# A GRU, attention and AUGRU kernel: five softmax blocks, an even pooling rate, products on GpSimd, attention ahead of the gates, and half-width chains

## The chip, the cores and the metric

The kernel runs on one core of a Trainium2 chip. The metric is the device time of one execution in microseconds (us).

Engines are named as in the profile: PE is TensorE (matmuls), PEld its weight loads, DVE is VectorE, ACT is ScalarE, POOL is GpSimd, and SP only issues transfers. "x2" behind a group is its number of instructions. An `a<-b` names the output and an input of an instruction.

## The reference, cut to what matters

A batch of 1024 histories of 100 steps goes through a GRU. All its states ("keys") are scored against one item per history by a small network. A masked softmax over the 100 steps weighs the keys into `pooled`. A second recurrence (AUGRU) runs over the keys again, its update gate scaled by `pooled`.

```python
# one GRU step
r = sigmoid(i_r + h_r); z = sigmoid(i_z + h_z); n = tanh(i_n + r * h_n)
h_new = (1.0 - z) * n + z * h
# attention over all steps
feat  = concat([keys, q, keys - q, q * keys])
score = mlp(feat, [W0, W1, W2], relu); score = where(mask == 1, score, -inf)
attn  = softmax(score, axis=1)
pooled = einsum('bt,btd->bd', attn, keys); att_seq = pooled.T[:T]
# one AUGRU step
u = a_t * sigmoid([h, x] @ Wu + bu); r = sigmoid([h, x] @ Wr + br)
h_new = (1.0 - u) * h + u * tanh([h * r, x] @ Wh + bh)
# ... masked mean of the history, then a final network of three layers
```

No AUGRU step can start before the softmax over all 100 steps is known and pooled. That is the seam in the middle of the kernel.

## The kernel before

The batch is cut in two halves of 512 columns, so that TensorE works on one half while the vector engines work on the other. A tick is one pass of the loop, with one step of each half; I call one step of one half a half-step (7.72 us of TensorE work in the GRU). The second half runs five ticks later (`LAG = 5`). Scores are collected in blocks, each with its own softmax and a running rescaling of `pooled`. After a block's softmax its rows stand in `todo`, and `pool` takes some of them in every step: a weight row and a key tile are loaded, multiplied and added.

```python
ENDS = (48, 92, T)
# ... in gru(), after the gates of a step
            d = wp.tile([P, HB], F32, name="d")
            nc.vector.tensor_sub(d, h if t else h0, pi)
            nc.vector.tensor_mul(d, pz, d)
            nc.vector.tensor_add(hn, pi, d)
            nc.gpsimd.tensor_mul(m, x, m)                    # masked history sum
            nc.gpsimd.tensor_add(hist[:, cols], hist[:, cols], m)
            nc.sync.dma_start(out=keys_d[t][:, cols], in_=hn)
# ... attend(): three matmuls a step, the second of them on kq
                kq = wp.tile([P, HB], F32, name="kq")
                nc.vector.tensor_mul(kq, self.h, item[:, self.cols])
                parts += [(wk, self.h), (wkq, kq)]
# ...
            nc.sync.dma_start(out=self.s_b[s - a0 : s - a0 + 1, :], in_=mv[SC : SC + 1, :])
            if s == ENDS[self.block] - 1:
                self.softmax()
# ... pool()
                nc.sync.dma_start(out=eb, in_=e_d[j][row, self.cols].partition_broadcast(P))
                # ...
                nc.sync.dma_start(out=k, in_=keys_d[t][:, self.cols])
                if t == 0:
                    nc.vector.tensor_mul(acc, k, eb)
                else:
                    nc.vector.tensor_mul(eb, k, eb)
                    nc.vector.tensor_add(acc, acc, eb)
# ... the loop
        for half, s in now:
            if 0 <= s < T:
                half.gru(s)
            elif T + GAP <= s < 2 * T + GAP:
                half.augru(s - T - GAP)
        for half, s in now:
            if 0 <= s < T:
                half.attend(s)
                half.pool(2 if len(half.todo) > T - s else 1)
            elif s == T:
                half.attend(T)
                half.attend(T + 1)
                half.pool(len(half.todo))
                half.weights()
```

## Time and profile before

| | before |
|---|---|
| time, median of 3 runs | 2873.81 us (2870.04 to 2875.78) |
| span of the profiled execution | 2876.6 us |
| TensorE busy | 93% |
| VectorE, GpSimd busy | 64%, 28% |

The prediction shows the lines of this profile. A busy share is read with care here. PE's busy time includes matmuls that run slowly, and their ends are modelled. So I count **TensorE loss**: the length of a stretch, less 0.4288 us for each 512-column matmul instruction in it, half of that for one of 256 columns, and 0.1 us for a transpose (two transposes in a row start 0.11 us apart in the median). The prediction took a transpose like a full instruction; that is 16 us (48 x 0.33) of the difference between its 265.7 and the 285.3 below. The other 4 us are nine instructions that lie across a cut and were counted on both sides.

### The profile page before, as it was taken

The numbers are of one execution on the slowest core, as the hardware profiler recorded it, in microseconds if no ns is written. First come the engines' busy times: TensorE is split into PE (matmuls) and PEld (weight loads), VectorE is DVE, ScalarE is ACT, GpSimd is POOL, SyncE is SP. The second block draws the span as 40 slices with busy tenths as digits, with TensorE's granted clock in tenths as the row PEclk, the third lists the DMA queues.
The fourth block names the chain that finished last, engine by engine and source line by source line (L and its number), as shares of the span: only waits on it lengthen the run. The fifth ranks groups of instructions, "written<-read, shape, count | busy, mean of one in ns | idle before, by whom it ended". The sixth has DMA issues, their size and how long they took to land.

```text
span 2876.6 us, 22338 instructions
## 1 busy us (share of the span) xinstructions
PE 2669.4 (93%) x6080; PEld 1150.3 (40%) x6080; DVE 1843.4 (64%) x2674; ACT 945.5 (33%) x1431; POOL 809.9 (28%) x615
## 2 busy tenths in 40 slices
PE   6999999999999988999998847499999999999998
PEld 2444444444434333444443312144444444444443
DVE  4666666666678998766666988655555555555553
ACT  2333333333333222333333312133333333333333
POOL 3333333333333332333332300022222222222221
PEclk8999999999999999999999978699999999999999
DMA  6332323222245777433334777733333333333331
GB/s 196 99 99 95 103 95 103 93 99 99 96 135 188 236 240 224 158 100 102 106 100 134 237 237 253 227 102 103 102 103 102 102 102 102 102 102 102 103 101 42
DMA packets 213650, 375.69 MB, mean 131 GB/s; under 512 B 31568, under 2 KB 32436, under 8 KB 213524
## 3 DMA queue, kind: packets, MB, share of 16 engines
q1 hardware_dynamic: 213524, 374.27, 40.9%
q8 instruction: 47, 0.77, 0.1%
q14 instruction: 79, 0.65, 0.1%
HBM read 320.08 MB, written 53.67 MB: 130 GB/s over the span
## 4 chain that ended last, share of the span: by engine, by line
PE 64%; DVE 20%; DMA 8%; issue 5%; ACT 3%; SPq 1%; POOL 1%; DVEq 0%; ACTq 0%; POOLq 0%
PE ps L189 18%; PE pm L237 10%; PE pu L348 6%; PE pr L348 6%; PE ph L348 6%; PE pr L350 6%; PE ph L350 6%; PE pu L350 6%; DVE d L218 3%; DMA k<-keys_d 3%; DVE hn L219 3%; DVE eb L318 3%; DMA eb<-e_d 3%; DVE u L209 2%; DVE d L217 2%
## 5 line engine op out<-in xcount | busy, mean ns | idle before, releaser
L189 PE MATMUL ps<-x,wih 128*128 128x512 f32 x1200 | 586.9, 597 | 0.0
L189 PE MATMUL ps<-hn,whh 128*128 128x512 f32 x1188 | 584.3, 599 | 1.8 <-DVE hn L219 1.8
L220 POOL TENSOR_TENSOR m<-x,m 128x512 f32<-128x512 f32 x200 | 262.7, 1313 | 1085.9 <-DMA x<-in_hist_x 1054.3
L362 POOL TENSOR_TENSOR u<-u,at 128x512 f32<-128x512 f32 x200 | 254.3, 1272 | 877.1 <-ACT u L361 865.1
L366 DVE TENSOR_TENSOR ph<-ph,hn 128x512 f32<-128x512 f32 x198 | 138.4, 699 | 450.5 <-ACT ph L364 450.3
L189 PEld LDWEIGHTS ps<-x,wih 128*128 128x128 f32 x1200 | 230.1, 192 | 291.3 <-issue 282.2
L189 PEld LDWEIGHTS ps<-hn,whh 128*128 128x128 f32 x1188 | 228.3, 192 | 289.9 <-issue 286.9
L237 PE MATMUL pm<-hn,wk 128*128 128x512 f32 x400 | 219.7, 632 | 95.0 <-DVE hn L219 94.8
L243 ACT ACTIVATE mv<-f 128x512 f32<-128x512 f32 x204 | 128.5, 630 | 540.9 <-DVE f L241 531.6
L221 POOL TENSOR_TENSOR hist<-hist,m 128x512 f32<-128x512 f32 x200 | 287.6, 1438 | 15.7
L215 ACT ACTIVATE ps<-ps,bih 128x512 f32<-128x512 f32 x200 | 132.4, 662 | 423.1 <-DVE ps L214 423.0
L348 PE MATMUL pr<-k,wr 128*128 128x512 f32 x396 | 203.4, 595 | 46.6 <-DMA k<-keys_d 46.6
L209 DVE SCALAR_TENSOR_TENSOR u<-ps,bhh,r 128x512 f32<-128x512 f32 x198 | 147.5, 745 | 144.6 <-PE ps L189 138.0
L237 PE MATMUL pm<-kq,wkq 128*128 128x512 f32 x400 | 216.5, 624 | 11.6 <-DVE kq L231 11.0
L241 DVE TENSOR_TENSOR f<-pm,q 128x512 f32<-128x512 f32 x204 | 139.7, 685 | 132.2 <-PE pm L237 132.0
L357 ACT ACTIVATE pr<-pr,br 128x512 f32<-128x512 f32 x198 | 131.1, 662 | 276.1 <-PE pr L350 276.1
L237 PE MATMUL pm<-mv,w 128*128 128x512 f32 x404 | 210.8, 604 | 2.6 <-ACT mv L243 2.6
L350 PE MATMUL pr<-hn,wr 128*128 128x512 f32 x396 | 204.1, 597 | 9.1 <-DVE hn L368 9.1
L217 DVE TENSOR_TENSOR d<-hn,ps 128x512 f32<-128x512 f32 x198 | 135.6, 685 | 115.1 <-ACT ps L215 115.1
L361 ACT ACTIVATE u<-pu,bu 128x512 f32<-128x512 f32 x200 | 137.3, 687 | 214.6 <-PE pu L350 214.6
L348 PE MATMUL pu<-k,wu 128*128 128x512 f32 x400 | 205.2, 594 | 0.0
L350 PE MATMUL ph<-r,wh 128*128 128x512 f32 x396 | 202.7, 593 | 2.4 <-DVE r L358 2.4
(93 smaller groups left out, 2936.5 us busy)
## 6 DMA issues: line engine op xcount, KB each, us to landing
k<-keys_d SPq DMA_DIRECT2D x400, 256.0 KB
eb<-e_d SPq DMA_DIRECT2D x206, 256.0 KB
x<-in_hist_x SPq DMA_DIRECT2D x200, 256.0 KB
m<-mask_d SPq DMA_DIRECT2D x200, 256.0 KB
keys_d<-hn SPq DMA_DIRECT2D x200, 256.0 KB
at<-att_d SPq DMA_DIRECT2D x200, 256.0 KB
s_b<-mv SPq DMA_DIRECT2D x200, 2.0 KB
item<-in_item SPq DMA_DIRECT2D x1, 512.0 KB
```

The costliest lines, as they stand in the source:

```text
L189: nc.tensor.matmul(p, lhsT=w[:, g, :], rhs=v, start=(n == 0), stop=(n == len(parts) - 1),)
L209: nc.vector.scalar_tensor_tensor(out=u, in0=ph, scalar=bhh[:, 2:3], in1=r, op0=ALU.add, op1=ALU.mult)
L217: nc.vector.tensor_sub(d, h if t else h0, pi)
L220: nc.gpsimd.tensor_mul(m, x, m)
L221: nc.gpsimd.tensor_add(hist[:, cols], hist[:, cols], m)
L237: nc.tensor.matmul(p, lhsT=w, rhs=v, start=(n == 0), stop=(n == len(parts) - 1))
L241: nc.vector.tensor_add(f, p, q0[:, self.cols])
L348: nc.tensor.matmul(p, lhsT=w[:, 1, :], rhs=k, start=True, stop=v is None)
L350: nc.tensor.matmul(p, lhsT=w[:, 0, :], rhs=v, start=False, stop=True)
L361: nc.scalar.activation(u, pu, AF.Sigmoid, bias=later["bu"])
L362: nc.gpsimd.tensor_mul(u, u, at)
L366: nc.vector.tensor_sub(ph, ph, h)
```

## The change

It is meant to take TensorE's idle time out of the seam and the start: five blocks that shrink, so that few rows are left when the GRU ends; rows pooled at an even rate; the row's product on GpSimd and `kq` too, to relieve VectorE; each half's attention directly ahead of its own gates; and, where one half runs alone, two chains of 256 columns.

```diff
-ENDS = (48, 92, T)
+ENDS = (44, 72, 88, 96, T)
@@ start: first weights, then the first x; reciprocals on a small tile, through memory
+    x_first = xp.tile([P, HB], F32, name="x")
+    nc.sync.dma_start(out=x_first, in_=a["hist_x"][0][:, :HB])
@@ gru(): the step's chain is run per part of the columns
+            for c in parts:
+                self.gru_chain(t, x[:, c], h[:, c] if t else h0[:, c], hn[:, c])
@@ attend()
-                nc.vector.tensor_mul(kq, self.h, item[:, self.cols])
+                nc.gpsimd.tensor_mul(kq, self.h, item[:, self.cols])
@@ pool()
-                    nc.vector.tensor_mul(eb, k, eb)
+                    nc.gpsimd.tensor_mul(eb, k, eb)
                     nc.vector.tensor_add(acc, acc, eb)
@@ the loop
+        for half, other in ((first, second), (second, first)):
+            s = tick - LAG * half.i
+            o = tick - LAG * other.i
+            alone = not (0 <= o < T or T + GAP <= o < 2 * T + GAP)
+            parts = quarters if alone else whole
+            if 1 <= s <= T:
+                half.attend(s - 1)
+            # ... last attention layers at s == T
+            if 0 <= s < T:
+                half.gru(s, parts)
+            elif T + GAP <= s < 2 * T + GAP:
+                half.augru(s - T - GAP, parts)
+            if 0 <= s < T:
+                left = next(e for e in ENDS if e > s - 2) - s + 2
+                half.pool(-(-len(half.todo) // left))
```

Cut: the augru chains, which follow the pattern of the gru's, more buffers (x 5 to 6, pooling tiles 4 to 5, own rings for AUGRU loads), and the reciprocals' transfers.

More of the change, by code (lines that the diff above doesn't have):

```diff
@@ L65 @@
     att_d = dram.tile([T, B], F32, name="att_d")
+    rlen_d = dram.tile([P, NG], F32, name="rlen_d")
     def load(name, shape, src=None, dt=F32):
@@ L73 @@
     wih = load("wih", [P, 3, P])
-    whh = load("whh", [P, 3, P])
+    xp = ctx.enter_context(tc.tile_pool(name="xp", bufs=6))
+    x_first = xp.tile([P, HB], F32, name="x")
+    nc.sync.dma_start(out=x_first, in_=a["hist_x"][0][:, :HB])
     bih = load("bih", [P, 3])
     bhh = load("bhh", [P, 3])
+    whh = load("whh", [P, 3, P])
     pre = ctx.enter_context(tc.tile_pool(name="pre", bufs=1))
@@ L120 @@
     y = const.tile([1, B], F32, name="y")
-    xp = ctx.enter_context(tc.tile_pool(name="xp", bufs=5))
     hp = ctx.enter_context(tc.tile_pool(name="hp", bufs=8))
@@ L125 @@
     sp = ctx.enter_context(tc.tile_pool(name="sp", bufs=2))
-    kp = ctx.enter_context(tc.tile_pool(name="kp", bufs=4))
+    kp = ctx.enter_context(tc.tile_pool(name="kp", bufs=5))
     ps = ctx.enter_context(tc.tile_pool(name="ps", bufs=6, space=PSUM))
@@ L159, in load_later @@
             later[n] = load(n, shape)
-        len_i = pre.tile([P, B], I32, name="len_i", tag="once2")
-        nc.sync.dma_start(out=len_i, in_=a["len_i"].partition_broadcast(P))
-        length = const.tile([P, B], F32, name="length")
+        len_i = pre.tile([T, B], I32, name="len_i", tag="once2")
+        nc.sync.dma_start(out=len_i, in_=a["len_i"].partition_broadcast(T))
+        length = const.tile([T, B], F32, name="length")
         nc.vector.tensor_copy(length, len_i)
         later["length"] = length
+        len_g = pre.tile([P, NG], I32, name="len_g")
+        nc.sync.dma_start(out=len_g, in_=a["len_i"].rearrange("(p g) -> p g", p=P))
+        rlen_g = pre.tile([P, NG], F32, name="rlen_g")
+        nc.vector.tensor_copy(rlen_g, len_g)
+        nc.vector.reciprocal(rlen_g, rlen_g)
+        nc.sync.dma_start(out=rlen_d, in_=rlen_g)
     class Half:
@@ L174, in __init__, with gru @@
             self.todo = []
-        def gru(self, t):
+        def gru(self, t, parts):
             cols = self.cols
-            x = xp.tile([P, HB], F32, name="x")
-            nc.sync.dma_start(out=x, in_=a["hist_x"][t][:, cols])
+            if t or self.i:
+                x = xp.tile([P, HB], F32, name="x")
+                nc.sync.dma_start(out=x, in_=a["hist_x"][t][:, cols])
+            else:
+                x = x_first
             m = xp.tile([P, HB], F32, name="m")
@@ L184, in gru, with gru_chain @@
             hn = hp.tile([P, HB], F32, tag="h", name="hn")
+            for c in parts:
+                self.gru_chain(t, x[:, c], h[:, c] if t else h0[:, c], hn[:, c])
+            nc.gpsimd.tensor_mul(m, x, m)
+            nc.gpsimd.tensor_add(hist[:, cols], hist[:, cols], m)
+            nc.sync.dma_start(out=keys_d[t][:, cols], in_=hn)
+            self.h = hn
+        def gru_chain(self, t, x, h, hn):
+            n = x.shape[-1]
             def gate(g, parts):
-                p = ps.tile([P, HB], F32, tag="g", name=f"ps{g}")
-                for n, (w, v) in enumerate(parts):
+                p = ps.tile([P, n], F32, tag="g", name=f"ps{g}")
+                for j, (w, v) in enumerate(parts):
                     nc.tensor.matmul(
@@ L192, in gate @@
                         rhs=v,
-                        start=(n == 0),
-                        stop=(n == len(parts) - 1),
+                        start=(j == 0),
+                        stop=(j == len(parts) - 1),
                     )
@@ L199, in gru @@
             pr = gate(0, both)
-            r = wp.tile([P, HB], F32, name="r")
+            r = wp.tile([P, n], F32, tag="r", name="r")
             nc.scalar.activation(r, pr, AF.Sigmoid, bias=brz[:, 0:1])
@@ L206, in gru @@
             nc.scalar.activation(pz, pz, AF.Sigmoid, bias=brz[:, 1:2])
-            u = wp.tile([P, HB], F32, name="u")
+            u = wp.tile([P, n], F32, tag="u", name="u")
             if t:
@@ L215, in gru @@
             nc.scalar.activation(pi, pi, AF.Tanh, bias=bih[:, 2:3])
-            d = wp.tile([P, HB], F32, name="d")
-            nc.vector.tensor_sub(d, h if t else h0, pi)
+            d = wp.tile([P, n], F32, tag="d", name="d")
+            nc.vector.tensor_sub(d, h, pi)
             nc.vector.tensor_mul(d, pz, d)
             nc.vector.tensor_add(hn, pi, d)
-            nc.gpsimd.tensor_mul(m, x, m)
-            nc.gpsimd.tensor_add(hist[:, cols], hist[:, cols], m)
-            nc.sync.dma_start(out=keys_d[t][:, cols], in_=hn)
-            self.h = hn
         def attend(self, t):
@@ L326, in weights @@
                 out=att,
-                in0=later["length"][:T, self.cols],
+                in0=later["length"][:, self.cols],
                 scalar=step[:T, :],
@@ L333, in weights, with augru, augru_chain @@
             nc.sync.dma_start(out=att_d[:, self.cols], in_=att)
-        def augru(self, t):
+        def augru(self, t, parts):
             cols = self.cols
-            wr, wu, wh = later["wr"], later["wu"], later["wh"]
-            at = kp.tile([P, HB], F32, name="at")
-            nc.sync.dma_start(out=at, in_=att_d[t, cols].partition_broadcast(P))
-            k = kp.tile([P, HB], F32, name="k3")
-            nc.sync.dma_start(out=k, in_=keys_d[t][:, cols])
-            h = self.h if t else None
-            hn = hp.tile([P, HB], F32, tag="h", name="hn3")
+            at = kp.tile([P, HB], F32, name="at", bufs=4)
+            nc.sync.dma_start(out=at, in_=att_d[t, cols].partition_broadcast(P))
+            k = kp.tile([P, HB], F32, name="k3", bufs=4)
+            nc.sync.dma_start(out=k, in_=keys_d[t][:, cols])
+            hn = hp.tile([P, HB], F32, tag="h", name="hn3")
+            for c in parts:
+                h = self.h[:, c] if t else None
+                self.augru_chain(k[:, c], at[:, c], h, hn[:, c])
+            self.h = hn
+        def augru_chain(self, k, at, h, hn):
+            wr, wu, wh = later["wr"], later["wu"], later["wh"]
+            n = k.shape[-1]
             def gate(w, v, name):
-                p = ps.tile([P, HB], F32, tag="g", name=name)
+                p = ps.tile([P, n], F32, tag="g", name=name)
                 nc.tensor.matmul(p, lhsT=w[:, 1, :], rhs=k, start=True, stop=v is None)
@@ L353, in augru @@
             r = None
-            if t:
+            if h is not None:
                 pr = gate(wr, h, "pr")
-                r = wp.tile([P, HB], F32, tag="r", name="r3")
+                r = wp.tile([P, n], F32, tag="r", name="r3")
                 nc.scalar.activation(pr, pr, AF.Sigmoid, bias=later["br"])
@@ L359, in augru @@
             pu = gate(wu, h, "pu")
-            u = wp.tile([P, HB], F32, tag="u", name="u3")
+            u = wp.tile([P, n], F32, tag="u", name="u3")
             nc.scalar.activation(u, pu, AF.Sigmoid, bias=later["bu"])
@@ L364, in augru @@
             nc.scalar.activation(ph, ph, AF.Tanh, bias=later["bh"])
-            if t:
+            if h is not None:
                 nc.vector.tensor_sub(ph, ph, h)
@@ L370, in augru @@
                 nc.vector.tensor_mul(hn, u, ph)
-            self.h = hn
         def features(self):
             cols = self.cols
-            rlen = wp.tile([P, HB], F32, name="rlen")
-            nc.vector.reciprocal(rlen, later["length"][:, cols])
-            nc.vector.tensor_mul(hist[:, cols], hist[:, cols], rlen)
+            rlen = kp.tile([P, HB], F32, tag="eb", name="rlen")
+            nc.sync.dma_start(
+                out=rlen,
+                in_=rlen_d.rearrange("p g -> (p g)")[cols].partition_broadcast(P),
+            )
+            nc.gpsimd.tensor_mul(hist[:, cols], hist[:, cols], rlen)
             cross = const.tile([P, HB], F32, name=f"cross{self.i}")
@@ L423, in predict @@
             )
-    halves = [Half(i) for i in range(NH)]
-    for tick in range(2 * T + GAP + LAG):
+    whole, quarters = (ts(0, HB),), (ts(0, HB // 2), ts(1, HB // 2))
+    first, second = (Half(i) for i in range(NH))
+    for tick in range(2 * T + GAP + LAG + 1):
         if tick == 2:
             load_later()
-        now = [(half, tick - LAG * half.i) for half in halves]
-        for half, s in now:
-            if 0 <= s < T:
-                half.gru(s)
-            elif T + GAP <= s < 2 * T + GAP:
-                half.augru(s - T - GAP)
-        for half, s in now:
-            if 0 <= s < T:
-                half.attend(s)
-                half.pool(2 if len(half.todo) > T - s else 1)
-            elif s == T:
+        for half, other in ((first, second), (second, first)):
[5 more added lines that the diff above has]
+                half.attend(s - 1)
+            if s == T:
                 half.attend(T)
                 half.attend(T + 1)
+            if 0 <= s < T:
[5 more added lines that the diff above has]
+                half.pool(-(-len(half.todo) // left))
+            elif s == T:
                 half.pool(len(half.todo))
@@ L445 @@
                 half.features()
-            elif s == 2 * T + GAP - 1:
+            elif s == 2 * T + GAP:
                 half.predict()
```

## The prediction

> **What bounds the kernel now.** I read the page first (busy shares, then the rows of forty slices), then a table of stretches cut where those rows change, then groups by shape for durations, then the timeline at the places where TensorE stops.
>
> From the page:
>
> ```profile
> PE 2669.4 (93%) x6080; PEld 1150.3 (40%) x6080; DVE 1843.4 (64%) x2674; ACT 945.5 (33%) x1431; POOL 809.9 (28%) x615
> PE   6999999999999988999998847499999999999998
> PEclk8999999999999999999999978699999999999999
> GB/s 196 99 99 95 103 95 103 93 99 99 96 135 188 236 240 224 158 100 102 106 100 134 237 237 253 227 102 103 102 103 102 102 102 102 102 102 102 103 101 42
> ```
>
> TensorE is the engine to beat. Its row dips in slice 0, slices 13 to 15 and 22 to 25; the last two are where the traffic doubles, which is where attention pooling runs. The table of stretches (busy time and instruction count of each engine, clock, DMA share, GB/s):
>
> ```profile
> 0.00:72.00 72.00, 48.73 (x89) 19.52 (x90) 33.54 (x48) 14.59 (x22) 28.27 (x33) 0.88 0.62 196
> 72.00:792.00 720.00, 698.85 (x1604) 300.73 (x1603) 465.68 (x627) 233.24 (x359) 241.23 (x179) 1.00 0.30 98
> 792.00:1224.00 432.00, 397.06 (x889) 166.83 (x889) 365.76 (x529) 128.98 (x199) 137.92 (x96) 0.98 0.62 196
> 1224.00:1512.00 288.00, 286.67 (x663) 124.26 (x662) 182.85 (x257) 97.53 (x148) 99.83 (x74) 1.00 0.33 102
> 1512.00:1872.00 360.00, 240.78 (x526) 100.90 (x525) 283.82 (x453) 83.20 (x125) 61.31 (x45) 0.84 0.68 217
> 1872.00:2808.00 936.00, 936.00 (x2183) 414.35 (x2182) 487.81 (x728) 365.67 (x546) 229.98 (x182) 1.00 0.33 102
> 2808.00:2876.60 68.60, 61.32 (x135) 23.74 (x133) 23.96 (x35) 22.29 (x34) 11.41 (x9) 0.95 0.12 39
> ```
>
> The AUGRU stretch (1872 to 2808) is full: 936 us / 2183 instructions = 0.4288 us for each, the pitch of a 512-column matmul instruction (each matmul call is two). Counting instructions at that pitch, rather than the modelled busy time, gives TensorE's loss per stretch: 33.8, 32.2, 50.8, 3.7, 134.5, 0 and 10.7 us, together 265.7. So TensorE's work is 2876.6 - 265.7 = 2610.9 us, a floor this change doesn't lower. It can only win back losses. Half of them lie in 1512 to 1872, where the halves go from GRU to AUGRU. From the timeline there:
>
> ```profile
> 1726.93 2.07 PE L237 MATMUL pm<-hn,wk 128*128 128x512 f32 x2 [17.54 <-DVE hn L219]
> 1840.99 2.08 PE L348 MATMUL pr<-k,wr 128*128 128x512 f32 x2 [46.58 <-DMA k<-keys_d]
> ```
>
> TensorE waits 17.5 us for a state whose vector steps are queued between pooling steps, then 46.6 us for a key load of the AUGRU queued behind pooling loads. By the code, pooling is one row a step, two late; 35 rows are left when a half's last block adds 10 entries, and all 45 go at once. An entry loads 512 KB, and DMA moved at most 254 GB/s: 45 x 524288 B / 254 GB/s = 93 us.
>
> **What the skill says.** The Trainium skill, "SBUF — State Buffer", section "Who interferes with whom": a VectorE instruction with two SBUF inputs and a GpSimd instruction that reads SBUF exclude each other through a shared port, and the second waits for the first. The trace agrees. VectorE first, then GpSimd:
>
> ```profile
> 400.14 1.53 DVE L231 TENSOR_TENSOR kq<-hn,item 128x512 f32<-128x512 f32 x1
> ```
>
> ```profile
> 399.86 1.27 POOL L220 TENSOR_TENSOR m<-x,m 128x512 f32<-128x512 f32 x1 [6.19 <-DMA x<-in_hist_x]
> 401.20 1.60 POOL L221 TENSOR_TENSOR hist<-hist,m 128x512 f32<-128x512 f32 x1
> ```
>
> The kq product, 0.69 us when alone, takes 1.53 because the GpSimd multiply holds on until 401.13; the next GpSimd step is stretched to 1.60 in turn. The means by shape say it happens often:
>
> ```profile
> L231 DVE TENSOR_TENSOR kq<-hn,item 128x512 f32<-128x512 f32 x200 | 191.8, 959 | 5.0
> L318 DVE TENSOR_TENSOR eb<-k,eb 128x512 f32<-128x512 f32 x198 | 154.7, 793 | 42.6 <-DMA k<-keys_d 23.2 <-DMA eb<-e_d 19.0 <-issue 0.3
> L319 DVE TENSOR_TENSOR pooled<-pooled,eb 128x512 f32<-128x512 f32 x198 | 151.5, 767 | 1.0
> L221 POOL TENSOR_TENSOR hist<-hist,m 128x512 f32<-128x512 f32 x200 | 287.6, 1438 | 15.7
> ```
>
> "GPSIMD Engine Reference", section "3.1 Elementwise — side-by-side cycle accounting", puts a two-input add at 1.96 times VectorE's time; here 1.27 against 0.69 us, a ratio of 1.84. "TensorE: Matmul & The Clock Gate", section "What's actually happening", says the array falls to half clock after an idle window of about 3.4 us; the trace agrees: the instructions after the long waits above are some 0.85 us apart instead of 0.43. So an idle gap costs more than itself.
>
> **The change, part by part.**
>
> *Start (33.8 us lost).* The first gate matmuls begin at 13.0 us, after mask, item and attention weights; now x comes right after the first weights, so they can begin near 6 us (my choice). Two reciprocals leave VectorE; they stood in the second step's chain:
>
> ```profile
> 32.38 3.34 DVE L377 RECIPROCAL rlen<-length 128x512 f32<-128x512 f32 x1
> 35.63 0.62 DVE L219 TENSOR_TENSOR hn<-ps,d 128x512 f32<-128x512 f32 x1
> ```
>
> A GRU step alone at full width takes 9.5 to 9.9 us (state to state, 47.5, 56.9, 66.8), against 18 x 0.4288 = 7.72 us of TensorE work. As two chains one works while the other waits, so about 8 us. I put the remaining loss at 16.
>
> *Steady GRU before pooling (32.2).* Once each tick TensorE waits for hn or kq, since attention of both halves stands behind the gates of both. With attention(s-1) and gates of one half in a row, the other half has 7.72 us of work as cover. From the start of the reset gate's sigmoid to hn a chain took 5.3 us (52.37 to 57.62), 3.4 of it beside the half's own remaining gates. kq on GpSimd adds 1.27 - 0.69 = 0.6 us and possibly a wait of two GpSimd steps, 2.5 us: it still fits. Stretch four, nearly the same work, lost only 3.7 in 288 us. I take 12.
>
> *Pooling during the GRU (50.8 + 3.7).* The bound in 792 to 1224 was VectorE, 365.8 of 432 us busy and over 64 of 72 at its height. It now has u, two adds, sub, mul and f, 4.19 us a half-step, plus 0.69 a row. But pooling lasts from tick 46 to 100 at about two rows a half-step. I take 42, which includes the two more softmaxes per half with their transposes, table switches and waits.
>
> *GRU to AUGRU (134.5).* The blocks of 8 and 4 leave by the code 4 rows plus 6 entries: 10 instead of 45, 21 us of loads instead of 93. What stays is serial: three attention layers, score row, softmax, write and read of its weights, ten entries, write and read of att. Before, the second half took from 1757 to 1786 us up to the copy of the weights; with loads and ten entries I make it some 45 us, against which stand the other half's steps, about 4 x 5.15 us and whatever the scheduler can bring forward. I take 32.
>
> *End (10.7).* AUGRU steps alone took 6.9 us, of which 12 x 0.4288 = 5.15 is TensorE's. The final network stays as serial as it is. I take 8.
>
> *Added TensorE work.* 18 lone steps turn 12 gate instructions into 24 of half width, 432 in all. A weight load takes 0.19 us and half the pitch is 0.214, so I allow 0.01 us each, 4 us; four more softmaxes with eight transposes near 0.12 us, 4 us.
>
> Sum: 2610.9 + 16 + 12 + 42 + 32 + 8 + 8 = 2729 us of span; runs were 2.8 us below the profiled span, so 2726. I say 2725.
>
> **The rivals.** First, *the shared port becomes the bound in pooling*. Per half-step with two rows GpSimd has five instructions, 5 x 1.27 = 6.35 us, and the two sums on VectorE each take 0.69 of the same port: 7.73 us, against TensorE's 7.72. For it: the stretched instructions above. Against: not every step takes two rows, and pooling spans most of a thousand us. If it holds, with kq waiting behind products, pooling loses 80 to 110 us and the time is 2770 to 2795. Second, *DMA*: a half-step with two rows moves 7 tiles of 262144 B in 7.72 us, 238 GB/s, near the 254 seen. GpSimd in order then stalls on a late row, holding kq; with the port full too, 2800. Third, *everything hides*: the interleaving works as in stretch four and the transitions cost under 20 us; losses near 55 in all, 2660. A fourth, that the idle is merely moved (the scheduler hoists pooling as before, so the even rate does nothing), is partly true already: rows ran at four a tick, not two. But with 10 entries at the end the 93 us of loads can't return.
>
> **Range and chances.** The transition's gain alone (about 100) makes 2775; to miss 2% (2816) almost all other gains would have to be spent by the port. Eight in ten: 2660 to 2795. Faster by over 2%: 0.94; within 2%: 0.05; slower: 0.01.
>
> **What would show it.** Right: the same table with 72 to 720 at 98% or more; no TensorE wait over 15 us near the transition; no reciprocal of 3 us; GpSimd above 75% busy from about 730 to 1600 us with DMA at 200 to 240 GB/s; sums on VectorE longer than 0.77 us in the mean; first gates before 8 us. Wrong: pooling taking 60 us or more from TensorE, long waits for kq on GpSimd, half-width gates spaced well over 0.22 us, or a new wait on key loads at the transition.

## The result, and the profile after

The changed kernel takes **2883.55 us** in the median of 4 runs (2880.96 to 2884.86). The kernel before took 2872.53 (2870.04 to 2875.78) beside it. The ratio is 1.0037, with a 95% interval of 1.0019 to 1.0054. The prediction said 2725.

From the page of the changed kernel, first the busy shares, then TensorE, its granted clock and the traffic in forty slices:

```profile
PE 2693.1 (93%) x6322; PEld 1202.6 (42%) x6322; DVE 1649.3 (57%) x2399; ACT 966.1 (34%) x1497; POOL 1304.9 (45%) x1024
PE   7999999999897879989889887899999999999999
PEclk8999999999999999999999999899999999999999
GB/s 205 106 103 103 102 103 103 101 104 104 166 179 208 222 191 115 104 162 151 210 201 131 179 159 170 177 105 102 101 103 102 103 102 102 102 103 102 102 103 44
```

The deep dips of slices 22 to 25 are gone, and so are the bursts above 230 GB/s. The longest waits of TensorE at the seam, 17.54 and 46.58 us before, are now these (total us, times, longest):

```profile
PE ps L211 <- DVE hn L241: 7.6, 3, 7.1
PE pr L374 <- DVE hn L392: 7.0, 1, 7.0
```

In their place shallow dips to 7 and 8 run from slice 10 to slice 25. TensorE's busy share is the same 93%.

To compare the kernels stretch by stretch, I cut each trace where TensorE had done the same work as the kernel before at 72, 791.5, 1224, 1511.5 and 1872 us. In the kernel after these are the following times (columns: length, then busy time and instructions of PE, PEld, DVE, ACT and POOL, then clock, DMA share, GB/s):

```profile
0.00:69.40 69.40, 48.06 (x142) 31.09 (x143) 27.59 (x68) 17.67 (x37) 33.67 (x38) 0.88 0.65 201
69.40:778.30 708.90, 695.08 (x1611) 305.70 (x1611) 394.99 (x557) 238.85 (x362) 354.85 (x280) 0.99 0.34 110
778.30:1236.40 458.10, 403.52 (x883) 169.04 (x882) 278.35 (x367) 126.13 (x197) 283.35 (x217) 0.96 0.51 166
1236.40:1589.70 353.30, 309.77 (x682) 129.26 (x681) 235.29 (x314) 99.17 (x153) 222.57 (x169) 0.95 0.55 175
1589.70:1879.00 289.30, 238.45 (x627) 117.77 (x626) 200.43 (x314) 93.21 (x156) 168.57 (x127) 0.93 0.55 170
1879.00:2880.90 1001.90, 998.25 (x2384) 449.79 (x2382) 512.66 (x782) 391.07 (x593) 241.92 (x195) 1.00 0.31 98
```

TensorE's loss in each, by counting instructions, in us:

| work of | before | after | predicted after |
|---|---|---|---|
| start (before: 0 to 72) | 33.8 | 31.2 | 16 |
| GRU until pooling (72 to 791.5) | 32.5 | 22.0 | 12 |
| pooling beside the GRU (791.5 to 1511.5) | 60.6 | **152.0** | 42 |
| GRU to AUGRU (1511.5 to 1872) | 145.9 | 74.7 | 32 |
| AUGRU and end | 12.4 | 6.4 | 8 |
| sum | 285.3 | 286.4 | 110 |

So four stretches gained 90 us together and pooling lost 91. The remaining difference of the spans, 4.3 us, is 1.1 us of loss and 3.2 us for 32 more transposes.

The pooling rows of the table carry the signs: the clock is at 0.96 and 0.95. In these 811.4 us PE was busy 713.3 and had 659.4 us of work (811.4 - 152.0). So 98.1 us of the loss are idle time: 71 waits, 35 of them under 1 us, 19 over 2 us, the longest 4.0. The other 53.9 are matmuls that last longer than their pitch. Counted from the trace, 71 instructions in 19 places run at about half speed (mostly 0.85 us apart instead of 0.43) and make 32 of them; about 12 are the modelled ends of the last instruction before each wait, and 10 are spread thinly. So not every wait is followed by slow matmuls. GpSimd was busy 505.9 us, 62%, so on the mean of the stretch it was far from full. The two main waits of TensorE from 720 to 1700 us, of a like size, are the state and `kq`:

```profile
PE pm L255 <- DVE hn L241: 65.6, 34, 4.0
PE pm L255 <- POOL kq L249: 47.3, 46, 3.8
```

The groups by shape say what became slow (busy us, mean ns; then idle time before them and what ended it):

```profile
L336 POOL TENSOR_TENSOR eb<-k,eb 128x512 f32<-128x512 f32 x198 | 271.9, 1387 | 107.4 <-DMA k<-keys_d 70.9 <-DMA eb<-e_d 31.0 <-DMA m<-mask_d 2.0
L249 POOL TENSOR_TENSOR kq<-hn,item 128x512 f32<-128x512 f32 x200 | 260.2, 1301 | 118.6 <-DVE hn L241 113.6 <-PE ph L372 2.8 <-DVE e L297 1.8
L337 DVE TENSOR_TENSOR pooled<-pooled,eb 128x512 f32<-128x512 f32 x198 | 240.9, 1218 | 154.3 <-POOL eb L336 152.7
L200 POOL TENSOR_TENSOR m<-x,m 128x512 f32<-128x512 f32 x200 | 260.1, 1301 | 547.8 <-DMA x<-in_hist_x 526.2 <-DMA m<-mask_d 17.6 <-DMA keys_d<-hn 3.8
```

The sum on VectorE (L337) now takes 1218 ns, where it took 767. VectorE further idles 152.7 us in front of it, waiting for the product. And `kq`, which TensorE needs, stands in GpSimd's queue with `m` (L200) and the product (L336), which wait for loads. How these meet, from the timeline (start, length, instruction, and in brackets the wait before it):

```profile
966.21 4.16 POOL L336 TENSOR_TENSOR eb<-k,eb 128x512 f32<-128x512 f32 x3
966.30 2.07 PE L255 MATMUL pm<-kq,wkq 128*128 128x512 f32 x2 [3.48 <-POOL kq L249]
967.51 1.73 DVE L337 TENSOR_TENSOR pooled<-pooled,eb 128x512 f32<-128x512 f32 x1 [5.26 <-POOL eb L336]
```

TensorE waits 3.48 us for a `kq` that GpSimd made late (just before it stand an `m` that had waited 3.95 us for x, and `hist`). Its two matmuls then take 2.07 us where two in the running state take 1.02. VectorE has waited 5.26 us for the first of three products; then its sum is stretched to 1.73 us while the next two products run. Three theories fit this picture:

- **P, the port.** Sum and product exclude each other on the shared port of which the prediction speaks.
- **Q, the queue.** `kq` sits on TensorE's path but behind instructions that wait for loads.
- **S, the sum.** VectorE stops at a sum for a product not yet made, and the steps of the next state stand behind it. In a variant, **H**, the cause is that rows come in bunches of three or more a half-step.

### The profile page after: what moved, and what is told of

The parts are those of the page before. It is cut to its first block, busy times and chain, and to the rows that moved or that the text cites. A ratio compares the mean times of both kernels' runs of the same rounds, so it can differ in the third digit from the quotient of the medians.

```text
span 2880.9 us, 23257 instructions
## 1 busy us (share of the span) xinstructions
PE 2693.1 (93%) x6322; PEld 1202.6 (42%) x6322; DVE 1649.3 (57%) x2399; ACT 966.1 (34%) x1497; POOL 1304.9 (45%) x1024
## 5 line engine op out<-in xcount | busy, mean ns | idle before, releaser
L211 PE MATMUL ps<-x,wih 128*128 128x512 f32 (+1 forms) x1254 | 598.1, 585 | 15.7 <-DMA x<-in_hist_x 10.0
L386 POOL TENSOR_TENSOR u<-u,at 128x512 f32<-128x512 f32 (+1 forms) x209 | 257.0, 1230 | 773.7 <-ACT u L385 761.0
L211 PE MATMUL ps<-hn,whh 128*128 128x512 f32 (+1 forms) x1236 | 582.9, 580 | 7.6 <-DVE hn L241 7.6
L200 POOL TENSOR_TENSOR m<-x,m 128x512 f32<-128x512 f32 x200 | 260.1, 1301 | 547.8 <-DMA x<-in_hist_x 526.2
L390 DVE TENSOR_TENSOR ph<-ph,hn 128x512 f32<-128x512 f32 (+1 forms) x207 | 140.0, 676 | 448.5 <-ACT ph L388 448.3
L337 DVE TENSOR_TENSOR pooled<-pooled,eb 128x512 f32<-128x512 f32 x198 | 240.9, 1218 | 154.3 <-POOL eb L336 152.7
L336 POOL TENSOR_TENSOR eb<-k,eb 128x512 f32<-128x512 f32 x198 | 271.9, 1387 | 107.4 <-DMA k<-keys_d 70.9
L249 POOL TENSOR_TENSOR kq<-hn,item 128x512 f32<-128x512 f32 x200 | 260.2, 1301 | 118.6 <-DVE hn L241 113.6
L231 DVE SCALAR_TENSOR_TENSOR u<-ps,bhh,r 128x512 f32<-128x512 f32 (+1 forms) x206 | 149.6, 726 | 250.7 <-PE ps L211 232.3
L374 PE MATMUL pr<-hn,wr 128*128 128x512 f32 (+1 forms) x414 | 205.7, 579 | 7.1 <-DVE hn L392 7.0
L372 PE MATMUL pu<-k,wu 128*128 128x512 f32 (+1 forms) x418 | 207.1, 577 | 0.0
```

Of the source, the lines that this page charges most:

```text
L211: nc.tensor.matmul(p, lhsT=w[:, g, :], rhs=v, start=(j == 0), stop=(j == len(parts) - 1),)
L231: nc.vector.scalar_tensor_tensor(out=u, in0=ph, scalar=bhh[:, 2:3], in1=r, op0=ALU.add, op1=ALU.mult)
L249: nc.gpsimd.tensor_mul(kq, self.h, item[:, self.cols])
L336: nc.gpsimd.tensor_mul(eb, k, eb)
L372: nc.tensor.matmul(p, lhsT=w[:, 1, :], rhs=k, start=True, stop=v is None)
L374: nc.tensor.matmul(p, lhsT=w[:, 0, :], rhs=v, start=False, stop=True)
```

## The experiments

Each run was beside fresh runs of the kernel before. The text before each run is quoted. My first count of losses left out some half-width instructions; where an expectation speaks of a start that loses about 45 us, it is that count, 12 us too high. Its pooling and transition figures there are by time, not by equal work. The kernel before had medians from 2865 to 2876 us in the different rounds, so a difference of losses between rounds is uncertain by some us; the rounds of the first four experiments were the fastest. Outside every range for them came both products back on VectorE, both runs with rows spread evenly, the lag with PSUM, the score rows' control, and attention after the gates.

### kq back on VectorE

```diff
-                nc.gpsimd.tensor_mul(kq, self.h, item[:, self.cols])
+                nc.vector.tensor_mul(kq, self.h, item[:, self.cols])
```

> The changed kernel with only the attention product kq moved back to VectorE. In the pooling stretch (720 to 1700 us) the changed kernel loses about 190 us of TensorE. Theory Q (kq stands in GpSimd's queue behind pooling products that wait for loads, and TensorE waits for kq): the 93 us of waits for kq vanish, time 2780 to 2820. Theory S (VectorE's sums wait for GpSimd's products, with the new state queued behind them): little gain, 2850 to 2890. Theory P (the shared port is simply full): a middle gain, as VectorE's 0.69 us replaces GpSimd's 1.27 on the same port, 2820 to 2850. Steady GRU before pooling should go back from about 9 us lost to 15 to 30 if kq there mattered.

2844.18 us, ratio 0.9921 (0.9898 to 0.9945). Losses: start 22.4, GRU 9.7, pooling 137.9, transition 69.4. So `kq` on GpSimd costs the start 8.8 us and the GRU 12.3, but pooling only about 14 of its 91. From 720 to 1872 us TensorE still waited, as long for the state (45.0 us) as for `kq` (42.6), now on VectorE.

### The product back on VectorE

```diff
-                    nc.gpsimd.tensor_mul(eb, k, eb)
+                    nc.vector.tensor_mul(eb, k, eb)
```

> The changed kernel with only the pooling product moved back to VectorE; kq stays on GpSimd. Theory S (sums wait for products on another engine): the coupling is gone, loss in pooling falls from 190 to some 60 us, time 2750 to 2790. Theory Q (kq behind products): also a gain, as no product stands before kq, 2770 to 2810. Theory P: 2820 to 2850. Theory R (the five blocks and the even rate themselves cost): little gain, 2850 to 2890.

2794.73 us, 0.9746 (0.9727 to 0.9766). Pooling loses 87.9, transition 59.8. One line is worth 79 us in the loss from pooling on (226.7 to 147.7). The sum's mean fell from 1218 to 864 ns. The sum, and TensorE's two main waits from 720 to 1700 us:

```profile
L337 DVE TENSOR_TENSOR pooled<-pooled,eb 128x512 f32<-128x512 f32 x198 | 171.0, 864 | 0.5
PE pm L255 <- POOL kq L249: 47.0, 39, 3.9
PE pm L255 <- DVE hn L241: 18.4, 18, 2.6
```

This names the part but not the mechanism: it removes P, S and half of Q together. The waits say more: those for the state fall from 65.6 to 18.4 us, those for `kq` stay at 47. So what the product on GpSimd cost here seems to have come mainly through VectorE's chain, and less through products in front of `kq`; as one wait can hide another, this is not shown.

### Both back on VectorE

> The changed kernel with both products back on VectorE, all else kept. If the products on GpSimd are the whole loss in pooling, the loss falls to that of before or less (60 us) while the gains at the transition (97), the end (6) stay: 2750 to 2785. If blocks and rate cost by themselves (R), 2830 to 2880.

2812.14 us, 0.9815 (0.9785 to 0.9846): worse than the product alone. The start and GRU gain again (23.3 and 6.2), but pooling loses 119.5. Two products and a sum fill VectorE, and TensorE waited (720 to 1872 us) 45.9 us for states and 39.9 us, in 5 waits of up to 12.5, for score rows in front of a softmax. Offloading as such was not the error.

### The old three blocks in the new kernel

```diff
-ENDS = (44, 72, 88, 96, T)
+ENDS = (48, 92, T)
@@ loop
-                half.pool(-(-len(half.todo) // left))
+                half.pool(2 if len(half.todo) > T - s else 1)
```

> The changed kernel with the blocks (48, 92, 100) and the pooling rule of before; products stay on GpSimd. Theory R: the pooling stretch recovers; but 45 entries return at each half's end, so 2880 to 2930 with the loss at the transition over 100 us and that in 720 to 1700 below 120. Theories Q, S and P: the same entries cost the same wherever they are, loss in pooling stays at about 0.9 us an entry, and the transition loses over 100: 2920 to 2980.

2914.98 us, 1.0167 (1.0147 to 1.0187). Pooling 103.7, transition 173.1. The blocks do what they were made for: with them the transition loses 98 us less, and pooling 48 more. The sums in the traces agree: with the old blocks 87 rows are added up beside the GRU, in the changed kernel 135.

### Five blocks alone, in the kernel before

The same two edits the other way round, the rate's formula fitted to the old order, with nothing else of the change.

> The kernel before with the five blocks and the even rate alone. As predicted for that part: the transition's loss falls from 146 to 30 to 50, the pooling stretch takes one to three us more for each of four extra softmaxes, time 2770 to 2800. Theory R (blocks and rate cost in pooling by themselves): pooling loses 60 more, 2830 to 2850.

2845.35 us, 0.9899 (0.9884 to 0.9914). Pooling 98.4, transition 62.4. Against the kernel before, that is +37.8 and -83.5. So about 40 of the 91 us come with the blocks whatever engine multiplies. Counting sums in the pooling stretch shows what the blocks do there: they bring more rows at the same loss for each. The kernel before loses 60.6 us on 87 rows and this one 98.4 on 134, 0.70 and 0.73 us a row. With `kq` and the product on GpSimd it is 1.19 with the old blocks (103.7 on 87) and 1.13 in the changed kernel (152.0 on 135).

### Rows spread evenly by force

In the changed kernel the scheduler hoisted sums: VectorE ran five or six in a half-step right after a softmax, then about three, then none, though the code asks for an even rate. (In the kernel before it ran up to 5 in a half-step, and 13 at the seam.) Here each half-step's pooling may not be placed before that half-step's new state.

```diff
-            nc.vector.tensor_add(hn, pi, d)
+            self.last = nc.vector.tensor_add(hn, pi, d)
-                half.pool(-(-len(half.todo) // left))
+                with tc.issue_after(half.last.ins):
+                    half.pool(-(-len(half.todo) // left))
```

> The changed kernel, its pooling sums held in VectorE's queue behind the new state of the step in which the code places them, so that two a half-step is true of the queue and not only of the code (the queue of the changed kernel has three in most half-steps, five or six right after a softmax, then none). Theory H (three a half-step need (3+3) x 1.27 + 3 x 0.69 = 9.7 us of GpSimd and shared port against 7.72 us of TensorE; two need 7.73): loss in pooling 190 to some 80, time 2750 to 2790. Theory S (sums wait for products, whatever the rate): 2830 to 2870.

> The pooling product on VectorE as in the run before, and product and sum held to their step in the queue. Three a half-step are VectorE's 4.19 + 6 x 0.69 = 8.3 us, two 6.95 us, against 7.72. Theory H: pooling's loss falls from 134 to below 60, time 2700 to 2740. If the loss left with the product on VectorE is of the extra softmaxes and of kq's waits: 2770 to 2795.

With products on GpSimd: 2879.55 us, 1.0025 (1.0007 to 1.0043). Pooling 150.3, transition 76.5, as in the changed kernel. With products on VectorE: 2813.56, 0.9795 (0.9765 to 0.9825), where it was 0.9746 without the spreading. In the first, the sums did lie at one or two a half-step, save right after a softmax. TensorE's waits for the state nearly vanished from 720 to 1700 us (65.6 before the edit, 4.2 after), but this line of the waits took their place (total us, times, longest):

```profile
PE pm L255 <- POOL kq L249: 115.7, 64, 6.3
```

In the changed kernel that wait was 47.3 us. H falls. Two causes lie one behind the other: clear one wait and the next holds the same half-step.

### The accumulator in PSUM, and its control

An accumulator in PSUM leaves the sum with a single SBUF input; the rule in the prediction asks for two, so the sum should then leave the shared port alone. The accumulator takes two PSUM banks from the six of the gates; the control has four gate banks and the accumulator in SBUF as before.

```diff
-    pooled = const.tile([P, B], F32, name="pooled")
-    ps = ctx.enter_context(tc.tile_pool(name="ps", bufs=6, space=PSUM))
+    ps = ctx.enter_context(tc.tile_pool(name="ps", bufs=4, space=PSUM))
+    pq_ = ctx.enter_context(tc.tile_pool(name="pacc", bufs=1, space=PSUM))
+    pooled = pq_.tile([P, B], F32, name="pooled")
```

> The changed kernel with the running sum of pooling kept in two banks of PSUM (the gates get four banks instead of six), so that the sum has one SBUF input and leaves the shared port alone. Theory P (the port is what is lost): sums back from 1.22 to about 0.7 us, GpSimd's products from 1.39 to 1.27, time 40 to 70 us below the run with four banks alone. Theory S: sums short, but still waiting for products; under 25 us below it.

> Control for the run with the sum in PSUM: the changed kernel with four PSUM banks for the gates instead of six, nothing else. All theories: 2870 to 2910; the two chains of 256 columns may get worse with fewer banks.

Accumulator in PSUM: 2811.91 us, 0.9787 (0.9767 to 0.9807). Control: 2884.83, 1.0038 (1.0015 to 1.0061). The sum in the two, first with PSUM:

```profile
L338 DVE TENSOR_TENSOR pooled<-pooled,eb 128x512 f32<-128x512 f32 x198 | 137.9, 697 | 185.8 <-POOL eb L337 185.5
```

```profile
L337 DVE TENSOR_TENSOR pooled<-pooled,eb 128x512 f32<-128x512 f32 x198 | 242.8, 1228 | 154.4 <-POOL eb L336 152.6
```

The sum falls from 1228 to 697 ns, the product from 1387 to 1267. **Taking the sum off the port alone is worth 73 us** (2884.83 - 2811.91), 46.6 of them in pooling (152.1 to 105.5) and 22.8 in the transition. The wait for the product is no shorter, 185.5 against 152.6 us. So waiting as such isn't the main cost; S has little room.

### Sums a step behind their products

The product is made in one step of a half and summed in the half's next step, a whole tick later, so that it should be ready.

```diff
+            late, self.late = self.late, []
+            with tc.issue_after(hold.ins):        # after this half-step's new state
+                for kind, eb in late:
+                    add(kind, eb)
             # ... loads and product as before, then
-                    nc.vector.tensor_add(acc, acc, eb)
+                self.late.append((kind, eb))
```

(With nine `eb` buffers instead of five, and two little used tiles, `att` and `g1`, cut to one buffer each to make room. No control has these buffers without the lag.)

> The changed kernel, with each pooling sum queued on VectorE behind the new state of the half's next step, so a whole tick after its product on GpSimd (nine buffers for the weights' rows instead of five). VectorE should never wait for a product now. Theory S (waits of sums for products hold the new state): the loss in pooling falls from 190 to below 110, time 2780 to 2810. Theory P (the shared port): the sums still need the port, 2850 to 2880, with waits for kq left.

> Late sums as in the run before, and the running sum in PSUM: neither the wait nor the port is left. If port and coupling are the two causes of the loss: pooling loses 60 or less, time 2720 to 2760. If loads (DMA) or the extra softmaxes make the rest: 2780 to 2810, like the run with PSUM alone (2812).

Alone: 2859.77 us, 0.9952 (0.9929 to 0.9975). With the accumulator in PSUM: 2816.54, 0.9795 (0.9781 to 0.981), no better than PSUM without the lag. S is worth at most some 20 us of loss where the port is shared (286.4 to 265.9; that the buffers gave a part of it is not ruled out), and nothing where it isn't (217.5 to 215.4, and no gain in time). PSUM alone had waited for a gate bank (first two lines, from 720 to 1700 us), and the second run waits for `kq` on GpSimd instead (third line):

```profile
PE ps L212 <- DVE d L241: 62.1, 37, 4.1
PE pm L256 <- POOL kq L250: 8.8, 7, 2.1
PE pm L257 <- POOL kq L251: 89.0, 47, 4.5
```

Q now holds the half-step.

### PSUM accumulator and products on VectorE

> The running sum in PSUM and the pooling product on VectorE, kq on GpSimd: VectorE has 5.6 us a half-step at two rows and 6.95 at three, GpSimd 3.8. The product still takes the shared port (0.69 us), the sum doesn't, and no sum waits for GpSimd. Theory P and S together: 2745 to 2780, below the product on VectorE alone (2795). If four PSUM banks cost with this queue: 2790 to 2810.

**2756.85 us, 0.9596 (0.958 to 0.9612).** Pooling loses 57.1, on 133 rows 0.43 us a row, and the transition 49.2. The two edits take away over half of the loss in pooling and transition (226.7 to 106.3). The pooling stretches by equal work:

```profile
771.20:1179.30 408.10, 387.37 (x883) 165.89 (x882) 304.42 (x438) 127.85 (x197) 196.78 (x147) 0.99 0.58 185
1179.30:1487.80 308.50, 291.11 (x682) 125.21 (x681) 247.97 (x378) 102.11 (x155) 136.50 (x104) 0.99 0.62 202
```

The same 883 and 682 instructions take 408.1 and 308.5 us instead of 458.1 and 353.3, at a clock of 0.99. GpSimd is busy 333.3 of 716.6 us, 47%. VectorE is busier than in the changed kernel (552.4 us against 513.6) and TensorE loses less all the same. The five blocks now cost no more in pooling than the three did in the kernel before (60.6).

### The same, with the first steps' kq on VectorE

```diff
-                nc.gpsimd.tensor_mul(kq, self.h, item[:, self.cols])
+                (nc.vector if t < 6 else nc.gpsimd).tensor_mul(kq, self.h, item[:, self.cols])
```

> The sum in PSUM and the product on VectorE as in the fastest run, and kq on VectorE for the first six steps of each half, where GpSimd has a backlog of mask products in front of it. If that backlog is the loss at the start: 47.6 us lost in the first 72 fall to some 36, time 2740 to 2750. If late loads hold the start anyway: 2752 to 2760.

2754.78 us, 0.9582 (0.9547 to 0.9616). The start falls from 34.7 to 25.0, as it should, but the GRU stretch rises from 11.4 to 19.3. The two versions are not told apart. Either is about 4% faster than both kernels.

### Port, lag and queue together

PSUM accumulator, lagging sums, and `kq` on VectorE: P, S and Q should all be gone.

> As the run with late sums in PSUM (2816), but kq on VectorE throughout: nothing TensorE waits for stands in GpSimd's queue behind a load. Theory Q (kq behind products that wait for loads is the rest of the loss): the 89 us of waits for kq vanish, pooling's loss falls from 142 to below 90, time 2750 to 2785. If the rest is of the loads and softmaxes themselves: 2800 to 2820.

2806.14 us, 0.9761 (0.9725 to 0.9797). GRU 6.2, pooling 136.3, transition 39.6. In the steady half-steps Q is confirmed: from 905 to 930 us TensorE runs without a wait, 7.72 us a half-step, and the whole trace has 5.6 us of waits for `kq`. What takes it back are three waits for score rows in front of a softmax, 71.9 us in sum from 720 to 1700 and up to 33.7. This is one of them, in order of time, with the score rows' issues, and then what the transfer queue waited for from 1180 to 1217 us:

```profile
1199.06 0.50 SPq L271 DMA_DIRECT2D s_b<-mv  x1
1206.25 0.50 SPq L271 DMA_DIRECT2D s_b<-mv  x1
1213.28 0.50 SPq L271 DMA_DIRECT2D s_b<-mv  x1
1216.11 0.63 PE L284 MATMUL pt<-ident,s_b 28*128 28x28 f32 x4 [27.57 <-DMA s_b<-mv]
SPq L196 <- POOL hist L203: 25.2, 5, 5.2
```

TensorE stops at 1188.5 and the softmax's transposes begin at 1216.11. In between the one transfer queue still issues score rows, one each 7.2 us, though TensorE makes no new scores: the rows were several half-steps late. Each stands in that queue behind a mask load, which waits until GpSimd's `hist` frees its buffer (last line); and GpSimd waits 4 to 5 us each time for the x that the queue issues after that score row. Queue and GpSimd wait for each other in turn. No pooling load is issued in this stretch; by the code they stand in the same queue and can have made it late before.

### Score rows from another queue

The second run below is the control, where such waits hardly occurred.

```diff
-            nc.sync.dma_start(out=self.s_b[s - a0 : s - a0 + 1, :], in_=mv[SC : SC + 1, :])
+            nc.scalar.dma_start(out=self.s_b[s - a0 : s - a0 + 1, :], in_=mv[SC : SC + 1, :])
```

> The kernel with PSUM accumulator, lagging sums and kq on VectorE, but each score row is now sent from ScalarE's queue, which makes it, instead of from the one queue that also carries all pooling loads. If the score rows waited behind pooling loads that wait for a free buffer (theory D), TensorE's waits for the score row (71.9 us in the run without this) fall under 20 us and the time from 2806 to 2725 to 2765. If it is the ring of pooling tiles and the softmax's own steps that hold the blocks up, the waits move to another step of the softmax and the time stays at 2790 to 2815.

> The PSUM accumulator with products on VectorE (psum_prod, 0.9596 of before), score rows sent from ScalarE's queue. Here TensorE waited little for score rows, so theory D expects only a small gain: 2740 to 2757, ratio 0.953 to 0.959. If a DMA issue costs ScalarE's queue, on the path of every gate, as much as it saves, 2755 to 2775.

First: 2815.5 us, 0.979 (0.9758 to 0.9822). Second: 2819.65, 0.9814 (0.9784 to 0.9843), against 0.9596 without the edit (pooling now loses 119 us instead of 57). The first lies at the edge of the second alternative; the second fits neither. In the first, TensorE's waits for score rows do fall, from 73.6 to 12.1 us over the trace, so they were behind other transfers in the queue. But the time doesn't fall:

```profile
936.00 0.63 ACT L263 ACTIVATE mv<-f 128x512 f32<-128x512 f32 x1 [2.89 <-DVE f L261]
940.55 0.50 ACTq L271 DMA_DIRECT2D s_b<-mv  x1
941.11 0.69 ACT L225 ACTIVATE r<-ps,brz 128x512 f32<-128x512 f32 x1 [4.47 <-DMA eb<-e_d]
941.85 1.12 PE L213 MATMUL ps<-x,wih 128*128 128x512 f32 x2 [2.33 <-ACT r L225]
```

`mv` is done at 936.63, but the transfer of its row is issued only at 940.55, and the sigmoid behind it in ScalarE's queue starts at 941.11. TensorE pays 2.33 us. Waits of gate activations that ended with a landing pooling, key or mask transfer sum to 199 us on ScalarE (77.2, 51.1, 31.9, 23.9 and smaller ones); without the edit the trace has none. The wait has moved from the transfer queue to an engine on the path. Why the issue waited for the landing of a weight row isn't visible in the trace; that stays open. In the control these waits are small, 16 us in all, but TensorE's wait for `kq` rose from 32.9 to 93.5 us, with `m` on GpSimd waiting 413.9 us for x from 720 to 1700 instead of 295.8. Why x came later there I did not settle.

### No half-width chains

```diff
-            alone = not (0 <= o < T or T + GAP <= o < 2 * T + GAP)
+            alone = False
```

> The changed kernel with a lone half at full width, all else kept: what the two chains of 256 columns give. As predicted for that part: some 1.5 us a step over 18 lone steps, end and transition 15 to 30 us longer, time 2895 to 2910. If the chains give nothing because kq and the loads set the lone steps: 2880 to 2888.

2897.37 us, 1.0077 (1.004 to 1.0114). The start loses 40.0 instead of 31.2, AUGRU and end 11.8 instead of 6.4; the rest is as in the changed kernel. The chains are worth about 12 us of loss.

### Attention after the gates, as before

```diff
+        for half in (first, second):      # a second loop, after the gates of both
+            if 0 <= s < T:
+                half.attend(s)
```

(With the same rest of the loop; the attention lines leave the first one, and the rate counts one step later.)

> The changed kernel with attention of both halves after the gates of both, as before: what the new order gives. If it made the steady GRU full: 72 to 720 us loses 25 to 35 again instead of 9, time 2895 to 2915. If that came of kq on GpSimd or of the gates' chain alone: 2880 or less.

3291.99 us, 1.1448 (1.1398 to 1.1498), slower by far more than I expected. The GRU before pooling loses 283 us. From its timeline:

```profile
407.76 1.26 POOL L200 TENSOR_TENSOR m<-x,m 128x512 f32<-128x512 f32 x1 [2.97 <-DMA x<-in_hist_x]
410.32 1.26 POOL L249 TENSOR_TENSOR kq<-hn,item 128x512 f32<-128x512 f32 x1
411.64 2.08 PE L255 MATMUL pm<-kq,wkq 128*128 128x512 f32 x2 [3.95 <-POOL kq L249]
```

`kq` waits for `m` and `hist`, and `m` waited for x. TensorE waits about 4 us (3.6 to 4.3) in every tick here, then runs at half speed. This is Q in its pure form, with no pooling about: in five blocks alone, with the old order and `kq` on VectorE, this stretch lost 41 us. The order with attention ahead of the gates is what makes `kq` on GpSimd bearable at all; the two edits aren't independent.

## Why the prediction was wrong

The direction of the total was wrong: 2725 was predicted and 2883.55 came, outside the range of 2660 to 2795. Its sums come out when done again; of its readings one is off: in the row of slices, counted from 0, TensorE dips in 14 and 15 and in 21 to 25, where it says 13 to 15 and 22 to 25. By its own steps:

- **What bounds the kernel.** Right. TensorE's work stayed the same but for the transposes, and all movement was in its losses.
- **Start, 16.** Measured 31.2. "The first gate matmuls ... can begin near 6 us" held, as this line shows, and the reciprocals are off the path:

```profile
4.01 5.31 PE L211 MATMUL ps<-x,wih 128*128 128x256 f32 x12 [4.01 <-DMA x<-in_hist_x]
49.17 2.08 PE L255 MATMUL pm<-kq,wkq 128*128 128x512 f32 x2 [6.69 <-POOL kq L249]
```

  But "it still fits", for `kq` on GpSimd, did not: the second line waits 6.69 us for one that stands behind hoisted history products. With `kq` on VectorE the start loses 22.4.
- **GRU until pooling, 12.** Measured 22.0, of which 8.7 up to 720 us, before pooling begins; the rest is the beginning of pooling. The interleaving was right.
- **Pooling, "I take 42".** This is the step that failed: 152.0. It weighed VectorE's load only, and "about two rows a half-step" was an average. Three things were missing. The blocks bring rows of the seam into this stretch, 135 instead of 87 (+37.8, shown by five blocks alone). The shared port stretches sums and products (46.6 us here, shown by the accumulator in PSUM against its control). And one in-order queue on GpSimd holds loads' waits and TensorE's input (shown as a wait where P and S were gone: 89.0 us for `kq`, and none in steady half-steps after `kq` left the queue). What this queue costs in pooling is not shown in time: `kq` back on VectorE gave 14 us in the changed kernel, and with port and lag gone other waits took its place. These overlap, so their sum isn't the 91.
- **GRU to AUGRU, 32.** Measured 74.7. "No TensorE wait over 15 us" holds: the longest at this seam is 7.1 us. The gain of 71 was predicted as about 100. The last rows still share the port, and in the kernel with the PSUM accumulator and products on VectorE this stretch loses 49.2. The remaining 17 I can't assign.
- **End, 8.** Measured 6.4; half-width gates cost nothing extra, two instructions in 0.43 us.
- **The rivals.** The first, the shared port with `kq` behind products, named the mechanism, and its "against" (not every step takes two rows) is where it was weighed wrongly: it was given a loss of 80 to 110 and 2770 to 2795 us. But its form was wrong too. It asked whether port time exceeds TensorE's 7.72 us a half-step. GpSimd was busy 62% in pooling, not above 75, and the traffic was 166 to 175 GB/s, not 200 to 240. On the mean of the stretch it was not a matter of throughput, but of 71 single waits of up to 4.0 us, 98 us in all. "An idle gap costs more than itself" stood in the prediction and wasn't applied to pooling, where matmuls at half speed made about 32 of 152 us.
- **The chances.** The 0.94 rested on "the transition's gain alone makes 2775". The gain was real, but it was not independent of pooling: the rows that leave the seam are pooled somewhere.

What stays open: two ways to relieve one queue (score rows on ScalarE) put other waits in its place, and the version that clears the steady half-steps completely is not the fastest.

## What to carry to other kernels

Moving work to an idle engine isn't free when that engine's queue also holds an instruction that the bottleneck waits for: look at what stands in front of that instruction, and what it waits for, not at the engine's busy share. Where VectorE accumulates beside a GpSimd that reads SBUF, try the accumulator in PSUM: here it took the sum off the shared port, 1228 to 697 ns. And before counting the gain of emptying one stretch, follow where its work goes: it is added to the stretch before, which had its own bound.

## What the Trainium skill lacked or had wrong

- "SBUF — State Buffer", "Who interferes with whom": right on who excludes whom. With one input in PSUM the sum beside a busy GpSimd took 697 ns instead of 1228, and the product 1267 instead of 1387. What the page lacks is a size for a whole kernel: 73 us of 2885 here, for 198 sums.
- "TensorE: Matmul & The Clock Gate", "Architectural detail: the array is 16× 32×32, not 1× 128×128", says that the queue of each of GpSimd's cores is strictly first in, first out. The traces agree (`kq` behind an `m` that waits 2.97 us for x). It lacks what follows for a choice of engine: with GpSimd 62% busy in pooling, TensorE waited 47.3 us for `kq` in the changed kernel, and 115.7 with the rows spread evenly.
- "DMA: Bandwidth & Descriptors", "Issuing engines are not separate DMA queues", says that issuing from several engines only saves sequencer time. It lacks the risk: 200 small transfers issued from ScalarE, 0.50 us each, came with 199 us of waits of gate activations for transfers in one run, up to 10.2 us at once, and with 16 in another. Why is open.
- "TensorE: Matmul & The Clock Gate", "HAM oscillation — how this bites in real kernels", works out one case of a wait before every burst of matmuls. It lacks a size for short, irregular waits: here 71 of up to 4.0 us, 98 us in all, came with about 32 us of extra time of half-speed matmuls, in 19 places.
